# Whitening applied in 64x64 blocks with half-partition stores, and the first loads cut finer

## The chip, the cores and the metric

The kernel runs on one core of a Trainium2 chip. The core has a matrix engine (TensorE, PE in the profile), VectorE (DVE), ScalarE (ACT), GpSimd (POOL) and SyncE (SP), which here only issues DMA transfers. Data lie in SBUF, 128 partitions wide; products of PE arrive in PSUM, eight banks of 512 fp32 columns for each partition, and DVE or ACT copies them out ("eviction"). The metric is the time of one execution on the device in microseconds (us); smaller is better.

## The reference

The input x has 4 images of 256 channels and 64x64 pixels, fp32. Layer 0 computes 49 attention weights for each pixel and uses them to sum 49 shifted copies of x. Layer 1 whitens the result in 4 groups of 64 channels: mean and covariance over all images and pixels, five Newton steps towards an inverse square root, and one 64x64 matrix applied to each group.

```python
# layer 0
k = conv(x, w1, 7x7, dilation 2, padding 6) + b1        # w1: 128 x 256 x 7 x 7
k = conv(k, w2, 1x1) + b2                               # w2: 49 x 128
attn = softmax(k, axis=1)
xp = pad(x, 6)
shifts = stack([xp[:, :, 2*u:2*u+64, 2*v:2*v+64] for u in range(7) for v in range(7)], axis=1)
x = einsum('bkchw,bkhw->bchw', shifts, attn)
# layer 1, nc = 64 channels in a group, g = 4 groups
x = transpose(x, (1, 0, 2, 3)).reshape(g, nc, -1); m = x.shape[-1]
xc = x - x.mean(-1, keepdims=True)
Sigma = EPS * I + einsum('gdm,gem->gde', xc, xc) / m
rTr = (1.0 / einsum('gii->g', Sigma))[:, None, None]
Sigma_N = Sigma * rTr
P = I
for _ in range(5):
    P = 1.5 * P - 0.5 * (P @ P @ P) @ Sigma_N
xn = einsum('gde,gem->gdm', P * sqrt(rTr), xc)
out = xn * weight + bias                                # per channel
```

## The kernel before

Everything is fp32, and the stages follow one another with a good deal of overlap.

**Weights.** The two convolutions are merged: w2 times w1 gives a convolution from 256 channels straight to 49 taps. `w1` is loaded in four transfers (L183; two halves of 64 channels for each of the two channel blocks `cc` of 128), multiplied by `w2T` in 13 blocks of up to 10 channels (`CB`, L210; two products of 49 columns per block, one for each `cc`, into the two PSUM buffers `cv`) and evicted to `tapT`; each of the 49 taps is then transposed (L228) into `tap`. Evictions alternate between ACT and DVE (L202).

**First loads.** SP issues w1, then image 0 of x: even image rows into slot 0, odd rows into slot 1 (`load_x`, L129; four transfers of 1 MB, in rows of 256 bytes), then `gain` and `shift` (L191, L192). Every later store or load of SP stands behind these in SP's order, among them the store `gi` (L615) and the stores `gd` (L409). POOL clears some buffers once the weight pool is released, and then loads image 1 (slots 2 and 3, L129).

**Convolution.** The convolution of 7x7 taps is done by interpolation at 7 points in both directions (`row_eval`, `col_eval`, `conv_bank` at L491, `col_interp`, `row_interp`); some rows are convolved directly (`direct`, L597). Rows are handled in four phases: row `4q+a` of a slot belongs to phase `a`. For image 0 an order is written out by hand: DVE makes the first weights (`row_weights`, `weights`), then `row_eval(0, 1)`, which reads all four phases, then `col_eval`; PE does `direct0(INF, 0)`, which reads only phase 3 of both slots, then `direct0(0, 0)`, which reads phase 0, then the products of `conv_bank`. The transformed weights `wr` have one buffer for each of three banks of points, so DVE can write the next set only after PE has read the last.

**Attention, sum, moments.** Softmax, a move of the weights through DRAM into bands, the weighted sum (L926) and the moments (L976, into `sig`: 64x65 for each group) run under the convolution of the later images; a planner spreads them. Results of layer 0 stay in SBUF as the slots; three of them are spilled to DRAM and brought back at the end (`back`, L851).

**Whitening chain.** `whiten(cc)` runs for two halves of 128 channels, interleaved: two groups stand as two blocks on the diagonal of a 128x128 matrix. L1186 sums the diagonal by a product with the block matrix `blk`; `rtr` is its reciprocal, one number for each channel. The Newton steps are products of 128x128 (L1201, L1208). At the end `scale` holds gain times the square root of `rtr`, and `beta` comes from a product of the matrix with the mean (L1225).

**Apply** (L1246): for each image, half of the channels and 8 rows of a slot (512 columns), one product of the full 128x128 matrix; half of that matrix is zero. There are 64 products, one to each of three PSUM buffers `tp` in turn. The evictions multiply by `scale` and add `beta`, alternately on ACT (L1257) and DVE (L1261); two of them, for even and odd image rows, fill an `out` buffer of 128 partitions by 4 KB (four such buffers), and SP stores it in one transfer of 512 KB (L1265).

Of the kernel before, what the change touches and what calls it, by code (L numbers as in the profile page):

```python
# [9 lines left out]
F32 = mybir.dt.float32  # L10
AF = mybir.ActivationFunctionType
ALU = mybir.AluOpType
# [19 lines left out]
def kernel(  # L32
# [29 lines left out]
    nc = tc.nc  # L62
    B, C, H, W = x.shape
    P = 128
    NCC = C // P
# [4 lines left out]
    SH, SW = H // 2, W // 2  # L70
# [4 lines left out]
    GW = 64  # L75
# [15 lines left out]
    def pe(ins):  # L91
        return tc.keep_in_program_order(ins)

    const = ctx.enter_context(tc.tile_pool(name="const", bufs=1))
    work = ctx.enter_context(tc.tile_pool(name="work", bufs=2))
# [3 lines left out]
    ps_y = ctx.enter_context(tc.tile_pool(name="ps_y", bufs=1, space=bass.MemoryType.PSUM))  # L99
    ps_sg = ctx.enter_context(tc.tile_pool(name="ps_sg", bufs=1, space=bass.MemoryType.PSUM))  # L100

    def tp():
        return ps_tp.tile([P, 512], F32, tag="tp", name="tp")
# [18 lines left out]
    slots = {}  # L122
    store = []

    def load_x(s, k, queue):
        b, pr = divmod(k, 2)
        for cc in range(NCC):
            src = x[b, cc * P : (cc + 1) * P].rearrange("c (r two) w -> c r two w", two=2)
            queue.dma_start(store[s][:, cc], src[:, :, pr, :])  # L129
        slots[k] = store[s]  # L130
# [12 lines left out]
    nc.gpsimd.memset(b2_sb, 0.0)  # L143
    for h in range(2):
        nc.sync.dma_start(b2_sb[h * HB : h * HB + KT], b2.unsqueeze(1))
    gain_sb = const.tile([P, NCC], F32, name="gain_sb")
    shift_sb = const.tile([P, NCC], F32, name="shift_sb")

    w2T = w1p.tile([O1, P], F32, name="w2T")
    nc.gpsimd.memset(w2T, 0.0)  # L150
    t = tp()
# [3 lines left out]
    t = tp()  # L155
    nc.tensor.matmul(t[:, :1], w2T, b1_sb, start=True, stop=True)
    bias = const.tile([P, 1], F32, name="bias")
    nc.vector.tensor_tensor(bias, t[:, :1], b2_sb, ALU.add)

    cv_buf = []  # L160
    for k in range(2):
        t = ps_cv.tile([P, 512], F32, name=f"cv{k}")
# [13 lines left out]
    w1_sb = [w1p.tile([O1, P, KT], F32, name=f"w1_{cc}") for cc in range(NCC)]  # L176
# [1 line left out]
    tapT = w1p.tile([P, KT, P], F32, name="tapT")  # L178


    for c0 in range(0, P, P // 2):
        for cc in range(NCC):
            nc.sync.dma_start(  # L183
                w1_sb[cc][:, c0 : c0 + P // 2].rearrange("o c t -> o (c t)"),
                w1[:, cc * P + c0 : cc * P + c0 + P // 2].rearrange("o c u v -> o (c u v)"),
            )
    load_x(0, 0, nc.sync)
    load_x(1, 1, nc.sync)
    for cc in range(NCC):
        cs = slice(cc * P, (cc + 1) * P)  # L190
        nc.sync.dma_start(gain_sb[:, cc : cc + 1], gain[0, cs].rearrange("c a b -> c (a b)"))  # L191
        nc.sync.dma_start(shift_sb[:, cc : cc + 1], shift[0, cs].rearrange("c a b -> c (a b)"))  # L192


    n0, n3 = KS * NCC * 2 * KT, 3 * KS * NCC * KT
# [5 lines left out]
    def evict(k, o, i):  # L201
        (nc.vector.tensor_copy if k % 2 else nc.scalar.copy)(o, i)  # L202

    CB = 10
    for k, c0 in enumerate(range(0, P, CB)):
        n = min(CB, P - c0)
        t = cv_buf[k % 2]
        for cc in range(NCC):
# [5 lines left out]
                    start=True, stop=True,  # L214
# [8 lines left out]
    for k0 in range(0, KT, TB):  # L223
        n = min(TB, KT - k0)
        t = tp()
# [537 lines left out]
    for k in range(NY):  # L763
        a = bpool.tile([P, NCC, P // GW, GW + 1], F32, name=f"yt{k}")
# [369 lines left out]
                j += 1  # L1134
    apool.release()
    rpool = ctx.enter_context(tc.tile_pool(name="rp", bufs=1, reuse_waits="tile"))
    blk = rpool.tile([P, P], F32, name="blk")
    nc.gpsimd.memset(blk, 0.0)
    for g in range(P // GW):
# [10 lines left out]
    def square(name):  # L1150
        return bpool.tile([P, P], F32, tag="xb", name=name, bufs=4)

    wm, sc, beta = {}, {}, {}

    def whiten(cc):


        def evict(o, i):
            (nc.vector.tensor_copy if cc else nc.scalar.copy)(o, i)

        G = sig[:, cc]
        mu = work.tile([P, 1], F32, tag="mu", name=f"mu{cc}")
        nc.vector.tensor_scalar(mu, G[:, GW : GW + 1], 1.0 / NPIX, None, ALU.mult)
        D = square(f"D{cc}")
        nc.vector.tensor_scalar(D, ident, mu, None, ALU.mult)
        t = tp()
        nc.tensor.matmul(t[:, :P], blk, D, start=True, stop=True)
        nmu = work.tile([P, 1], F32, tag="nmu", name=f"nmu{cc}")
        nc.vector.tensor_scalar(nmu, mu, -1.0, None, ALU.mult)
        PS = rpool.tile([P, 2, P], F32, tag="PS", name=f"PS{cc}", bufs=2)  # L1170
        S = PS[:, 1]
        nc.vector.tensor_scalar(S, ident, EPS, None, ALU.mult)
        yield
        for g in range(P // GW):
            gs = slice(g * GW, (g + 1) * GW)
            nc.vector.scalar_tensor_tensor(
                S[gs, gs], G[gs, :GW], 1.0 / NPIX, S[gs, gs], ALU.mult, ALU.add
            )
        nc.vector.scalar_tensor_tensor(S, t[:, :P], nmu, S, ALU.mult, ALU.add)
        yield  # L1180
        dt_ = square(f"dt{cc}")
        nc.vector.tensor_tensor(dt_, S, ident, ALU.mult)
        dg = work.tile([P, 1], F32, tag="dg", name=f"dg{cc}")
        nc.vector.tensor_reduce(dg, dt_, AX.X, ALU.add)
        t = tp()
        nc.tensor.matmul(t[:, :1], blk, dg, start=True, stop=True)  # L1186
        yield
        rtr = work.tile([P, 1], F32, tag="rtr", name=f"rtr{cc}")
        nc.vector.reciprocal(rtr, t[:, :1])
        nc.vector.tensor_scalar(S, S, rtr, None, ALU.mult)  # L1190


        i15 = square(f"i15_{cc}")
        nc.vector.tensor_scalar(i15, ident, 1.5, None, ALU.mult)
        Pm = PS[:, 0]
        nc.vector.scalar_tensor_tensor(Pm, S, -0.5, i15, ALU.mult, ALU.add)
        yield

        for it in range(1, T_ITERS):
            t = tp()  # L1200
            nc.tensor.matmul(  # L1201
                t[:, : 2 * P], Pm, PS.rearrange("p a c -> p (a c)"), start=True, stop=True
            )
            sq = rpool.tile([P, 2, P], F32, tag="sq", name=f"sq{cc}_{it}", bufs=2)
            evict(sq.rearrange("p a c -> p (a c)"), t[:, : 2 * P])
            yield
            t = tp()
            nc.tensor.matmul(t[:, :P], sq[:, 0], sq[:, 1], start=True, stop=True)  # L1208
            nc.vector.tensor_scalar(Pm, Pm, 1.5, None, ALU.mult)
            yield  # L1210
            nc.vector.scalar_tensor_tensor(Pm, t[:, :P], -0.5, Pm, ALU.mult, ALU.add)
            yield


        q = work.tile([P, 1], F32, tag="q", name=f"q{cc}")
        nc.scalar.activation(q, rtr, AF.Sqrt)
        qi = work.tile([P, 1], F32, tag="qi", name=f"qi{cc}")
        nc.vector.reciprocal(qi, q)
        nc.vector.scalar_tensor_tensor(q, qi, rtr, q, ALU.mult, ALU.add)
        scale = work.tile([P, 1], F32, tag="scale", name=f"scale{cc}")  # L1220
        nc.vector.scalar_tensor_tensor(
            scale, q, 0.5, gain_sb[:, cc : cc + 1], ALU.mult, ALU.mult
        )
        t = tp()
        nc.tensor.matmul(t[:, :1], Pm, mu, start=True, stop=True)  # L1225
        yield
        bt = work.tile([P, 1], F32, tag="beta", name=f"beta{cc}")
        nc.vector.tensor_scalar(bt, t[:, :1], scale, -1.0, ALU.mult, ALU.mult)
        nc.vector.tensor_tensor(bt, bt, shift_sb[:, cc : cc + 1], ALU.add)
        wm[cc], sc[cc], beta[cc] = Pm, scale, bt  # L1230

    chains = [whiten(cc) for cc in range(NCC)]
# [1 line left out]
        pass  # L1234


    NT = 512
    TR = NT // W
    n = 0
    for b in (3, 2, 1, 0):  # L1240
        for cc in range(NCC):
            for q in range(SH // TR):
                st = rpool.tile([P, TR, 2, W], F32, tag="out", name=f"out_{b}_{cc}_{q}", bufs=4)
                for pr in range(2):
                    t = tp()
                    nc.tensor.matmul(  # L1246
                        t,
                        wm[cc],
                        slots[2 * b + pr][:, cc, q * TR : (q + 1) * TR, :].rearrange(
                            "p r w -> p (r w)"  # L1250
                        ),
                        start=True,
                        stop=True,
                    )
                    t3 = t.rearrange("p (r w) -> p r w", w=W)
                    if n % 2 == 0:
                        nc.scalar.activation(  # L1257
                            st[:, :, pr, :], t3, AF.Identity, bias=beta[cc], scale=sc[cc]
                        )
                    else:  # L1260
                        nc.vector.tensor_scalar(  # L1261
                            st[:, :, pr, :], t3, sc[cc], beta[cc], ALU.mult, ALU.add
                        )
                    n += 1
                nc.sync.dma_start(  # L1265
                    out[b, cc * P : (cc + 1) * P, 2 * q * TR : 2 * (q + 1) * TR, :],
                    st.rearrange("p r two w -> p (r two) w"),
                )


# [29 lines left out]
```

## Time and profile before

| | us |
|---|---|
| runs shown | 792.08, 794.63, 799.25 (median 794.63) |
| profiled execution, its own time | 793.55 |
| its span, first to last instruction | 791.8 |

| engine | busy us | share of the span | instructions |
|---|---|---|---|
| PE | 722.7 | 91% | 7444 |
| PE weight loads | 547.6 | 69% | 7444 |
| DVE | 625.9 | 79% | 1314 |
| ACT | 346.4 | 44% | 1018 |
| POOL | 34.1 | 4% | 46 |

The page gives busy time per engine, a chain of waits followed back from the last instruction, groups of instructions of one line ("operation output<-input, partitions x elements, xcount | busy, mean ns of one | idle before, and what ended it"), and DMA issues. An fp32 product appears as two records of matmul and two of weight load. The time line and the chain in order of time give "start us, length us, engine, line, operation, count", and in brackets the idle time before it and what ended that. A table by stage gives each engine's busy time in a stretch, the TensorE clock that was granted (1.00 is full), the mean busy share of the 16 DMA engines, and what they moved in GB/s. DMA moved 114.76 MB in all, at a mean of 145 GB/s; the times of its transfers are in the page's last part: the 32 stores of the output, 512 KB each, land 2.6 us after their issue (median), the four loads of w1 11.9 us, the four of image 0 22.8 us.

### The profile page before, as it was taken

Reading aid. Unit: us, or ns where it says so; the run is one execution under the profiler, and the core shown is the slowest. Engines: PE = TensorE matmul, PEld = TensorE weight load, DVE = VectorE, ACT = ScalarE, POOL = GpSimd, SP = SyncE. Lnnn points to the kernel's source line nnn. Section 1 sums busy time; section 2 is a strip of 40 time slices with the busy share of each in tenths; the row PEclk is TensorE's granted clock in tenths of the full one; section 3 lists DMA queues with packets and bytes.
Section 4 is the critical chain, followed back from the end, with each engine's and each line's share of the span. In section 5 each row is a group of like instructions: output and inputs, shape, how many; then the busy total and the mean of one; then the engine's idle time right before and its main releaser. Section 6 shows DMA issues by size and latency. Waiting matters only on the chain.

```text
span 791.8 us, 18445 instructions
## 1 busy us (share of the span) xinstructions
PE 722.7 (91%) x7444; PEld 547.6 (69%) x7444; DVE 625.9 (79%) x1314; ACT 346.4 (44%) x1018; POOL 34.1 (4%) x46
## 2 busy tenths in 40 slices
PE   4899969799799999989999999896999889998997
PEld 1349653265688887768899958795998768875443
DVE  2696999999888999979896899696979775545443
ACT  1313241125674444378543344765333573422443
POOL 0320000030000010001000100000000000000000
PEclk9999989999899999999999999998999999998999
DMA  8991110033654383048644720542431233381676
GB/s 331 226 297 58 42 72 36 0 107 121 187 182 147 114 313 81 19 153 265 202 124 147 247 66 8 155 161 84 143 87 30 48 113 126 106 298 53 265 301 283
DMA packets 58717, 114.76 MB, mean 145 GB/s; under 512 B 22615, under 2 KB 41736, under 8 KB 57352
## 3 DMA queue, kind: packets, MB, share of 16 engines
q1 hardware_dynamic: 54936, 94.71, 36.2%
q0 software_dynamic: 3696, 18.88, 7.1%
q8 instruction: 59, 0.97, 0.5%
q14 instruction: 26, 0.21, 0.1%
HBM read 66.23 MB, written 47.33 MB: 143 GB/s over the span
## 4 chain that ended last, share of the span: by engine, by line
PE 36%; DVE 29%; ACT 12%; DMA 5%; issue 4%; SPq 1%; DVEq 0%; ACTq 0%
PE y L926 11%; PE cv L491 8%; PE tp L1246 7%; ACT zt L837 6%; DMA sd<-zt 4%; DVE xh L296 3%; PE sig L976 3%; PE tp L897 3%; PE tp L955 3%; DVE zz L296 3%; DVE pv L296 2%; DVE rb L289 2%; ACT d L794 2%; DVE ct L296 2%; DVE pv L292 2%
## 5 line engine op out<-in xcount | busy, mean ns | idle before, releaser
L491 PE MATMUL cv<-xh,wr 128*49 128x128 f32 x4368 | 251.6, 276 | 6.6 <-DVE xh L296 6.5
L491 PEld LDWEIGHTS cv<-xh,wr 128*49 128x49 f32 x4368 | 245.3, 124 | 11.5 <-issue 9.1
L926 PE MATMUL y<-band,xb 128*128 128x224 f32 (+2 forms) x640 | 156.0, 383 | 17.4 <-ACT xb L905 15.2
L926 PEld LDWEIGHTS y<-band,xb 128*128 128x128 f32 x640 | 112.3, 198 | 40.2 <-ACT xb L905 18.1
L837 ACT COPY zt<-d 32x112 f32<-32x112 f32 (+1 forms) x224 | 62.8, 281 | 22.1 <-DMA sd<-zt 13.8
L897 PE MATMUL tp<-ident,slot 128*128 128x128 f32 x256 | 51.1, 303 | 15.0 <-ACT yt L963 15.0
L963 ACT COPY yt<-tp 128x256 f32<-128x256 f32 x128 | 45.4, 375 | 36.7 <-PE tp L955 35.7
L945 ACT ACTIVATE slot<-y,pivot 128x512 f32<-128x512 f32 x53 | 36.5, 736 | 52.3 <-PE y L926 52.3
L501 ACT COPY pv<-cv 113x486 f32<-113x486 f32 (+1 forms) x63 | 29.8, 473 | 63.7 <-PE cv L491 62.4
L897 PEld LDWEIGHTS tp<-ident,slot 128*128 128x128 f32 x256 | 40.3, 206 | 22.3 <-ACT yt L963 16.7
L955 PE MATMUL tp<-ident,slot 128*128 128x128 f32 x256 | 52.2, 300 | 3.6 <-ACT xb L905 1.2
L879 DVE STREAM_TRANSPOSE band<-band 128x960 f32<-128x960 f32 (+1 forms) x48 | 50.9, 1059 | 5.8 <-DMA band<-sd 5.7
L955 PEld LDWEIGHTS tp<-ident,slot 128*128 128x128 f32 x256 | 41.5, 205 | 13.6 <-issue 4.4
L1261 DVE TENSOR_SCALAR out<-tp,scale,beta 128x512 f32<-128x512 f32 x32 | 25.9, 810 | 29.5 <-PE tp L1246 29.5
L794 ACT ACTIVATE d<-tp,mx 128x49 f32<-128x49 f32 x128 | 36.9, 336 | 12.2 <-DVE mx L789 12.1
L1257 ACT ACTIVATE out<-tp,beta,scale 128x512 f32<-128x512 f32 x32 | 24.9, 778 | 32.0 <-PE tp L1246 32.0
L296 DVE SCALAR_TENSOR_TENSOR xh<-ct 128x512 f32<-128x512 f32 x42 | 27.9, 686 | 12.6 <-PE cv L491 12.4
L976 PE MATMUL sig<-yt 128*64 128x65 f32 x1024 | 37.5, 227 | 0.0
L976 PEld LDWEIGHTS sig<-yt 128*64 128x64 f32 x1024 | 33.0, 140 | 6.0 <-issue 4.5
L1246 PE MATMUL tp<-slot,PS 128*128 128x512 f32 x80 | 35.9, 593 | 0.0
L905 ACT COPY xb<-tp 128x256 f32<-128x256 f32 x87 | 30.6, 374 | 12.0 <-PE tp L897 11.2
L597 PE MATMUL cv<-slot,wi 128*49 128x496 f32 (+3 forms) x168 | 34.7, 570 | 0.0
(203 smaller groups left out, 991.7 us busy)
## 6 DMA issues: line engine op xcount, KB each, us to landing
out_dram<-out SPq DMA_DIRECT2D x32, 512.0 KB, 2.6
sd<-zt SPq DMA_DIRECT2D x16, 896.0 KB, 4.3
slot<-in_x_dram POOLq DMA_DIRECT2D x12, 1024.0 KB, 10.0
band<-sd SPq DMA_DIRECT2D x128, 84.0 KB, 2.1
wr<-gd SPq DMA_DIRECT2D x15, 588.0 KB, 4.0
wr<-gd SPq DMA_DIRECT2D x15, 490.0 KB, 3.5
w<-in_L_conv_w_dram SPq DMA_DIRECT2D x4, 1568.0 KB, 11.9
spill<-slot POOLq DMA_DIRECT2D x3, 2048.0 KB, 7.8
```

The costliest lines, as they stand in the source:

```text
L296: return in_turn(STT(o, a, f, b, ALU.mult, ALU.add))
L491: nc.tensor.matmul(cv[h * HB : h * HB + KT, k, sr : sr + n, sc : sc + n], wv[:, sc, sr, cc], xh[bc][:, :n, h * NCC + cc, :n], start=(j == ...
L794: nc.scalar.activation(d[:, h, i], lt[i // NI][:, i % NI, h, :KT], AF.Exp, bias=mx[:, i, h : h + 1], accum_out=s[:, h, i : i + 1],)
L837: nc.scalar.copy(o, i)
L879: nc.vector.transpose(f, f)
L897: nc.tensor.transpose(t[:, cc * P : (cc + 1) * P], xt[:, cc, CR * m : CR * (m + 1), bass.ds(pc, SW, 2)], ident,)
L926: nc.tensor.matmul(ps[:, cc, q0 - half * HALF : q1 - half * HALF, :], xb[:, cc * P : (cc + 1) * P], rhs, start=(k == 0), stop=(k == len(PI ...
L945: nc.scalar.activation(o, ps[:, cc], AF.Identity, bias=pivot[:, cc : cc + 1])
L955: nc.tensor.transpose(t[:, cc * P : (cc + 1) * P], yt[:, cc, CR * i : CR * (i + 1), bass.ds(pc, SW, 2)], ident,)
L963: nc.scalar.copy(yb.rearrange("p a g c -> p (a g) c")[:, :, :GW], t[:, :C].rearrange("p (e c) -> p e c", c=GW),)
L976: nc.tensor.matmul(sig[g * GW : (g + 1) * GW, cc], yb[:, cc, g, :GW], yb[:, cc, g], start=(count[0] == 0 and cc == 0), stop=(count[0] == 4 ...
L1246: nc.tensor.matmul(t, wm[cc], slots[2 * b + pr][:, cc, q * TR : (q + 1) * TR, :].rearrange("p r w -> p (r w)"), start=True, stop=True,)
```

## The change

1. **First weights.** w1 comes in five parts of 30, 30, 30, 20 and 18 channels for each `cc`, ten transfers for four.
2. **x of image 0** comes by row phases, phase 3 first, then 0, 1 and 2: 16 transfers of 256 KB for four of 1 MB.
3. **gain and shift** are laid out for groups of 64 channels (64 channels by 4 groups, twice, once for each half of the partitions) and are loaded by POOL's queue, ahead of POOL's clearing of buffers.
4. **Whitening chain.** `scale` and `beta` become 128x2 (one column for each group of the half, the same in both halves of the partitions). For that, the diagonal sum of each group is spread over all partitions by a product with a matrix of ones (`dgg`, `tg`, `rg`), and the product with the mean is made of four 64x64 products.
5. **Apply.** For 16 rows of a slot and both groups of a half, four products of 64x64 by 512 columns: group `g` reads partitions `64g` to `64g+63`, and 8-row piece `h` writes partitions `64h` to `64h+63` of bank `g`. So a bank holds one group, with its first 8 rows in the lower partitions and the next 8 in the upper. Three pairs of banks are used in turn (the former `y`, `cv`, and two `tp`). Evictions stay 128 partitions by 512. There are six `out` buffers for four, and each is stored in two transfers of 64 partitions, 256 KB.

```diff
-    for c0 in range(0, P, P // 2):
+    CB = 10
+    for c0, c1 in ((0, 3), (3, 6), (6, 9), (9, 11), (11, 13)):
+        c0, c1 = c0 * CB, min(c1 * CB, P)
         for cc in range(NCC):
             nc.sync.dma_start(
-                w1_sb[cc][:, c0 : c0 + P // 2].rearrange("o c t -> o (c t)"),
-                w1[:, cc * P + c0 : cc * P + c0 + P // 2].rearrange("o c u v -> o (c u v)"),
-            )
-    load_x(0, 0, nc.sync)
-    load_x(1, 1, nc.sync)
-    for cc in range(NCC):
-        cs = slice(cc * P, (cc + 1) * P)
-        nc.sync.dma_start(gain_sb[:, cc : cc + 1], gain[0, cs].rearrange("c a b -> c (a b)"))
-        nc.sync.dma_start(shift_sb[:, cc : cc + 1], shift[0, cs].rearrange("c a b -> c (a b)"))
+                w1_sb[cc][:, c0:c1].rearrange("o c t -> o (c t)"),
+                w1[:, cc * P + c0 : cc * P + c1].rearrange("o c u v -> o (c u v)"),
+            )
+
+    for pr in range(2):
+        slots[pr] = store[pr]
+    for a in (3, 0, 1, 2):
+        for pr in range(2):
+            for cc in range(NCC):
+                nc.sync.dma_start(
+                    store[pr][:, cc].rearrange("c (q a) w -> c a q w", a=4)[:, a],
+                    x[0, cc * P : (cc + 1) * P].rearrange(
+                        "c (q a two) w -> c two a q w", two=2, a=4
+                    )[:, pr, a],
+                )
+    for h in range(2):
+        hs = slice(h * GW, (h + 1) * GW)
+        for t, src in ((gain_sb, gain), (shift_sb, shift)):
+            nc.gpsimd.dma_start(t[hs], src[0].rearrange("(g c) a b -> c (g a b)", c=GW))
...
+        dgg = work.tile([P, P // GW], F32, tag="dgg", name=f"dgg{cc}")
+        nc.vector.tensor_scalar(dgg, blk[:, ::GW], dg, None, ALU.mult)
+        tg = tp()
+        nc.tensor.matmul(tg[:, : P // GW], ones, dgg, start=True, stop=True)
         rtr = work.tile([P, 1], F32, tag="rtr", name=f"rtr{cc}")
         nc.vector.reciprocal(rtr, t[:, :1])
         nc.vector.tensor_scalar(S, S, rtr, None, ALU.mult)
+        rg = work.tile([P, P // GW], F32, tag="rg", name=f"rg{cc}")
+        nc.vector.reciprocal(rg, tg[:, : P // GW])
...
-        nc.vector.scalar_tensor_tensor(q, qi, rtr, q, ALU.mult, ALU.add)
...
-        nc.tensor.matmul(t[:, :1], Pm, mu, start=True, stop=True)
+        nc.vector.tensor_tensor(qi, qi, rg, ALU.mult)
+        nc.vector.tensor_tensor(q, qi, q, ALU.add)
...
+        ts = [tp() for g in range(G2)]
+        for g in range(G2):
+            gs = slice(g * GW, (g + 1) * GW)
+            for h in range(2):
+                nc.tensor.matmul(
+                    ts[g][h * GW : (h + 1) * GW, :1], Pm[gs, gs], mu[gs],
+                    start=True, stop=True, skip_group_check=True,
+                )
...
+    def banks():
+        while True:
+            t = ps_y.tile([P, G2, NT], F32, tag="y", name="apply")
+            yield [t[:, g] for g in range(G2)]
+            yield cv_buf
+            yield [tp() for g in range(G2)]
...
-                    nc.tensor.matmul(
-                        t,
-                        wm[cc],
-                        slots[2 * b + pr][:, cc, q * TR : (q + 1) * TR, :].rearrange(
-                            "p r w -> p (r w)"
-                        ),
...
+                    ts = next(pair)
+                    for h in range(2):
+                        for g in range(G2):
+                            gs = slice(g * GW, (g + 1) * GW)
+                            pe(
+                                nc.tensor.matmul(
+                                    ts[g][h * GW : (h + 1) * GW],
+                                    wm[cc][gs, gs],
+                                    slots[2 * b + pr][
+                                        gs, cc, (q + h) * TR : (q + h + 1) * TR, :
+                                    ].rearrange("p r w -> p (r w)"),
...
-                nc.sync.dma_start(
-                    out[b, cc * P : (cc + 1) * P, 2 * q * TR : 2 * (q + 1) * TR, :],
-                    st.rearrange("p r two w -> p (r two) w"),
-                )
+                for g in range(G2):
+                    c0 = cc * P + g * GW
+                    for h in range(2):
+                        r0 = 2 * (q + h) * TR
+                        nc.sync.dma_start(
+                            out[b, c0 : c0 + GW, r0 : r0 + 2 * TR, :],
+                            st[g][h * GW : (h + 1) * GW].rearrange("p r two w -> p (r two) w"),
+                        )
```

## The prediction

> **What bounds the kernel now.** I read the page first: its chain of waits puts 36% of the span on TensorE (PE), 29% on VectorE (DVE), 12% on ScalarE (ACT), 5% on DMA. The diff touches only the two ends of the span, so I then read the chain in order of time and the time line there. Last stage, from the chain:
>
> ```profile
> 731.22 0.02 issue
> 731.24 0.30 DVE PS L1211
> 731.54 0.04 issue
> 731.59 0.38 PE tp L1225 x2
> 731.97 55.06 PE tp L1246 x128
> 787.03 0.03 issue
> 787.05 0.81 DVE out L1261
> ```
>
> One unbroken piece of PE is 55.06 us. 64 products of 128x128 by 512 columns make 128 records (two passes each), so a product costs 0.86 us. What runs beside it, from the table by stage (PE, PEld, DVE, ACT, POOL busy, clock, DMA share, GB/s) and the page's groups:
>
> ```profile
> 744.00:748.00 4.00, 4.00 (x11) 1.83 (x10) 2.05 (x3) 1.66 (x3) 0.00 (x0) 1.00 0.76 312
> 748.00:752.00 4.00, 4.00 (x10) 1.71 (x9) 2.00 (x3) 1.65 (x3) 0.00 (x0) 1.00 0.79 323
> L1261 DVE TENSOR_SCALAR out<-tp,scale,beta 128x512 f32<-128x512 f32 x32 | 25.9, 810 | 29.5 <-PE tp L1246 29.5
> L1257 ACT ACTIVATE out<-tp,beta,scale 128x512 f32<-128x512 f32 x32 | 24.9, 778 | 32.0 <-PE tp L1246 32.0
> ```
>
> DVE and ACT are half idle and wait for PE; DMA is next in line, three quarters busy.
>
> Start, from the time line:
>
> ```profile
> 12.98 13.59 PE L210 MATMUL cv<-w,w2T 128*49 128x490 f32 x50 [1.86 <-DMA w<-in_L_conv_w_dram]
> 32.99 1.92 PE L597 MATMUL cv<-slot,tap 128*49 128x512 f32 x6
> 37.18 11.64 PE L597 MATMUL cv<-slot,tap 128*49 128x512 f32 x48 [2.28 <-DMA slot<-in_x_dram]
> 60.81 23.03 PE L491 MATMUL cv<-xh,wr 128*49 128x128 f32 x409
> 66.41 0.36 DVE L289 TENSOR_TENSOR wr<-ct 128x196 f32<-128x196 f32 x1 [5.47 <-PE cv L491]
> ```
>
> PE gets its first full pair of weight parts at 12.98, although DMA has been full since 4 us. It does three products of the direct convolution at 33, then stands until x arrives at 37.18. The last line counts most: DVE, busy without a gap from 29.7 to 61, waits 5.47 us for PE, since its next weights go into a buffer that PE is reading. So up to 66.4 **PE leads and DVE has 5.5 us of slack**; from there to about 145 DVE leads.
>
> [...] The trace shows column pairs only: in the direct convolution (L597) two products of 49 columns take 0.80 us together, as one does. In steps of 10 ns, two of its records begin in the same step at 32.99, so the second product doesn't wait for the second pass of the first. No row tile is in the trace. [...] The change gives each channel group its own bank. [...] No 64-partition store is in the trace. [...] 439 GB/s while the weights load, and stretches at 426 to 442 inside single stores.
>
> **The change part by part.**
>
> *First weights.* Ten transfers of 0.45 to 0.75 MB replace four of 1.6 MB; the same 6.4 MB. The last byte lands near 20.4 as now (6.4 MB at 430 GB/s from 4.2 us = 19.1, plus 1.3 to land: a 512 KB store lands 2.6 us after issue, half of that is its bytes). Part one (1.5 MB) is there at about 8.8 instead of 12.98. Now 13 column blocks at 0.86 to 1.05 us each follow 12.98 and end at 27.1. Then, only the two blocks of part five lie after the last byte: 20.4 + 2 x 0.86 + 0.5 eviction = 22.7; if the first blocks run at a low clock, as the first does now (1.9 us), 23.5. I take **3.8 us earlier** for the L228 transposes and for DVE's weight sums behind them. Six more issues on SP at about 0.46 us lie under 15 us of transfers.
>
> *gain and shift.* Four issues leave SP, where they stand between 29.76 and 36.8 ahead of the gi and gd stores, for POOL, which is idle from 1.5 to 33. Their 1,024 four-byte elements fall among the first weights. An x row of 256 B costs an engine 15 ns (16,384 rows in 15.5 us over 16 engines); at that price 64 elements per engine delay the weights by 1 us. Bounds 0 and 2; inside the 3.8.
>
> *x by row phases.* 16 transfers of 256 KB for four of 1 MB, the same 256 B rows in another order. x moves at 280 GB/s: phase 3, which the first direct convolution needs, lands near 25, phase 0 near 29, all near 37 as now. POOL's loads for image 1 start about 4 us earlier, at 34, and overlap the end by a microsecond or two. DVE's row_eval needs all four phases and would start at 42.3 - 3.8 = 38.5: just covered. If x is late, DVE loses its 3.8, but not PE.
>
> *PE at the start.* Transposes end at 33.0 - 3.8 = 29.2. The 112 records of the two direct convolutions at 0.405 us a pair are 22.7 us, without the wait and without the half clock (0.50 at 38 to 40) after it. L491 begins at 51.9 instead of 60.81: 8.9 earlier. PE frees the weight buffer at 57.5, DVE is there at 61.0 - 3.8 = 57.2. So **8.5 us** of 66.4 go; 5.5 if DVE doesn't move at all, 9.5 at best. Instruction order behind this is the same on PE, DVE, POOL and SP, and ACT's early shifts (the acc eviction ahead of an xh copy) cover work needed only later, so I let the gain run through.
>
> *Whitening chain* (715.2 to 732). Added per half: a 128x2 multiply, a 128x128 product with one eviction, a 128x2 reciprocal in front of the first PS; at the end four 64x64 products for one, and three small DVE operations for two. L1186 took 0.40 us from product to DVE read, a small DVE operation 0.15 to 0.2. One product round and some four of these on the path, and a wait for the fourth of three tp banks: **1.3 us** more, bounds 0.3 and 2.5. The two sets of scale operations lie under the iteration.
>
> *Apply.* 128 products of 64x64, four in 0.86 us if all run at once: 32 x 0.86 = 27.6 us of PE for 55.1. Evictions stay 32 x 0.81 on DVE, 32 x 0.78 on ACT, 26 us each. SP issues 64 stores: 64 x 0.33 (a store's issue now) = 21 us. So DMA becomes the bound: 16.78 MB. A share of 0.76 at 312 GB/s means 410 at full share: 40.9 us. Before that, two rounds of PE, an eviction and the way to the first byte: 1.7 + 0.8 + 0.9 = 3.4 us; after the last byte 1.8 (now 790.0 to 791.8); a microsecond for gaps: 47.0 us. Now, from 731.8 to 791.8, it is 60.0. **13.0 us** less; bounds: 440 GB/s gives 15, 350 gives 7. Six output buffers at 1.28 us of transfer each hold 7.7 us, their round of two evictions, issue and landing is about 5, so they don't hold DMA up.
>
> Sum: -8.5 + 1.3 - 13.0 = **-20.2** on the profiled execution of 793.55 us (span 791.8 plus 1.75 around it): 773.4. It lies 1.1 under the median of 794.63, so I forecast **774.5**.
>
> **Rivals.** *A, row tiles don't run at once* (the change doesn't do what it says): pairs of columns alone make 64 x 0.86 = 55 us of PE again. The apply stage is then as now: 794.6 - 8.5 + 1.3 = 787. For: no row tile in the trace. Against: the independence of column tiles at 32.99[...]. *B, the start's gain is given back* before 145 us, or x comes late enough to hold PE too: 794.6 + 1.3 - 13.0 = 783. For: DVE and PE have less than a microsecond between them then. Against: 5.5 us of slack in DVE's wait. *C, slower: stores of 64 partitions move at half the rate*, 205 GB/s. Apply is 3.4 + 82 + 2 = 87 us for 60: 794.6 - 7.2 + 27 = 814. Break-even is an apply stage of 67 us, 271 GB/s; under 240 it is over 1% slower. For: the 32-partition band loads reach only 197 GB/s at a share of 0.8. Against: those are 84 KB each with short rows, paced by an issue of 0.42 us; the store keeps its 4 KB rows.
>
> **How the numbers follow.** Main case 0.63, B 0.14, A 0.12, C 0.07, rest 0.04. Main case's own bounds: 794.6 - 9.5 + 0.3 - 15 = 770 to 794.6 - 5.5 + 2.5 - 7 = 785. The range 769 to 788 takes in A and B and leaves out C. One per cent (7.9 us) is what can be told from no change: 786.7 divides. Faster: main, B, rest and a little of A: 0.82; same: 0.11; slower: 0.07.
>
> **What would show it.** Transposes ending near 29; no wait of PE for x; DVE's wait of 5.5 at L289 gone to below 1; L491 starting near 52; the apply products in about 28 us of PE work but spread over 43 by waits for evictions, with DVE and ACT waiting for the stores' buffers, and a DMA share near 1 at over 400 GB/s. Wrong if PE still runs without a gap through the apply stage (A), or if DMA shows a share near 1 at half the GB/s (C).

## The result, and the profile after

The changed kernel takes 828.99 us (median of 4 runs, 825.91 to 830.77) against 793.95 for the kernel before beside it: ratio 1.0426, 95% interval 1.0365 to 1.0487. It is slower by 4%, where 774.5 us was forecast. The profiled execution took 825.91 us, span 824.1.

Four points on the time line show where the time went: the first product of conv_bank, the first operation of whitening (mu), the first eviction of the apply stage, the end of the span.

| us | before | after | stage before | stage after | difference |
|---|---|---|---|---|---|
| conv_bank's first product | 60.0 | 66.5 | 60.0 | 66.5 | +6.5 |
| whitening begins | 716.4 | 741.0 | 656.4 | 674.5 | +18.1 |
| first apply eviction | 733.0 | 758.5 | 16.6 | 17.5 | +0.9 |
| end | 791.8 | 824.1 | 58.8 | 65.6 | +6.8 |

More than half of the loss lies in the long middle, which the diff doesn't touch. The start first, from the time lines of TensorE (PE), then VectorE (DVE) of the changed kernel (start, duration, engine, line, operation, count, idle time before it and what ended that):

```profile
9.74 13.76 PE L223 MATMUL cv<-w,w2T 128*49 128x490 f32 x50 [1.17 <-DMA w<-in_L_conv_w_dram]
29.91 11.59 PE L610 MATMUL cv<-slot,tap 128*49 128x512 f32 x56
41.33 11.55 PE L610 MATMUL acc<-slot,tap 128*49 128x512 f32 x56
66.47 8.73 PE L504 MATMUL cv<-xh,wr 128*49 128x128 f32 x106 [13.60 <-DVE xh L302]
```

```profile
59.58 2.36 DVE L302 TENSOR_TENSOR rb<-slot 128x1024 f32<-128x1024 f32 x2 [18.00 <-DMA slot<-in_x_dram]
```

PE did what was planned: weights from 9.74, both direct convolutions without a gap from 29.91. Then DVE stood for 18 us on x, and PE for 13.6 us on DVE. The DMA records between 40 and 44 us show what x was up against (packets, MB and share of 16 engines by queue; q0 is POOL's, q1 is SP's):

```profile
DMA packets 626, 0.87 MB, mean 217 GB/s; under 512 B 441, under 2 KB 441, under 8 KB 626
q0 software_dynamic: 197, 0.76, 86.4%
q1 hardware_dynamic: 429, 0.11, 18.9%
```

POOL is loading image 1 in records of about 4 KB, while the last rows of image 0 go by in 256 B: seven bytes of image 1 for one of image 0. From 46 to 48 us it is 99 records of 4096 B on POOL's queue against 99 of 256 B on SP's, from 46 to 58 us 630 against 637 in all, and the last part of image 0 lands only at 59.5. So x of image 0 had not come in before POOL started: its rate was 219 GB/s where the kernel before has 280 (between 24 and 30 us, first line before, second after):

```profile
DMA packets 6584, 1.68 MB, mean 280 GB/s; under 512 B 6584, under 2 KB 6584, under 8 KB 6584
```

```profile
DMA packets 5149, 1.31 MB, mean 219 GB/s; under 512 B 5148, under 2 KB 5148, under 8 KB 5148
```

The end: the chain of waits, then the table by stage (PE, PEld, DVE, ACT, POOL busy, clock, DMA share, GB/s), an eviction group and the list of DMA issues:

```profile
806.00 1.06 SPq L1327
...
807.15 0.69 SPq L1327
...
807.90 4.35 DMA out_dram<-out
```

```profile
764.00:768.00 4.00, 2.65 (x28) 0.84 (x24) 1.90 (x3) 1.52 (x3) 0.00 (x0) 1.00 0.84 275
768.00:772.00 4.00, 2.11 (x24) 0.71 (x20) 1.53 (x2) 1.43 (x2) 0.00 (x0) 1.00 0.84 269
```

```profile
L1318 DVE TENSOR_SCALAR out<-cv,scale,beta 128x512 f32<-128x512 f32 x11 | 8.8, 804 | 8.9 <-DMA out_dram<-out 8.9
```

```profile
out_dram<-out SPq DMA_DIRECT2D x64, 256.0 KB, 4.1
```

PE is no longer the bound: it is busy 2.1 to 2.7 us in each 4 and the evictions wait for stores. But the stores move 270 GB/s, not 410, and the chain runs through SP, where one issue takes 0.545 to 1.299 us (median 0.887) instead of 0.332. The 64 issues take 55.6 us in all and follow one another, from 760.1 to 819.6, with no pause over 0.3 us.

### The profile page after: what moved, and what is told of

Same layout as the page of the kernel before. It is cut to its first block, busy times and chain, and to the rows that moved or that the text cites. A ratio compares the mean times of both kernels' runs of the same rounds, so it can differ in the third digit from the quotient of the medians.

```text
span 824.1 us, 18802 instructions
## 1 busy us (share of the span) xinstructions
PE 712.7 (86%) x7588; PEld 539.5 (65%) x7588; DVE 625.7 (76%) x1322; ACT 344.6 (42%) x1018; POOL 36.8 (4%) x51
## 4 chain that ended last, share of the span: by engine, by line
PE 36%; DVE 24%; ACT 11%; SPq 6%; DMA 6%; issue 4%; DVEq 0%; ACTq 0%
PE y L939 13%; PE cv L504 11%; ACT zt L850 5%; SPq L1327 5%; DMA sd<-zt 3%; PE sig L989 3%; PE tp L910 3%; PE tp L968 3%; DVE xh L309 3%; DVE zz L309 2%; ACT d L807 2%; DMA band<-sd 2%; DVE pv L309 2%; DVE ct L309 1%; PE cv L610 1%
## 5 line engine op out<-in xcount | busy, mean ns | idle before, releaser
L504 PE MATMUL cv<-xh,wr 128*49 128x128 f32 x4368 | 254.9, 279 | 21.6 <-DVE xh L302 15.1
L504 PEld LDWEIGHTS cv<-xh,wr 128*49 128x49 f32 x4368 | 248.7, 126 | 26.5 <-ACT xh L475 14.4
L939 PE MATMUL y<-band,xb 128*128 128x224 f32 (+2 forms) x640 | 163.2, 397 | 18.6 <-ACT xb L918 16.4
L939 PEld LDWEIGHTS y<-band,xb 128*128 128x128 f32 x640 | 116.7, 205 | 44.1 <-ACT xb L918 19.4
L958 ACT ACTIVATE slot<-y,pivot 128x512 f32<-128x512 f32 x53 | 36.5, 734 | 59.6 <-PE y L939 59.5
L514 ACT COPY pv<-cv 113x486 f32<-113x486 f32 (+1 forms) x63 | 29.8, 473 | 71.8 <-PE cv L504 65.4
L968 PEld LDWEIGHTS tp<-ident,slot 128*128 128x128 f32 x256 | 41.5, 206 | 13.7 <-issue 4.5
L309 DVE SCALAR_TENSOR_TENSOR pv<-pv 113x162 f32<-113x162 f32 x105 | 33.7, 321 | 1.0
L302 DVE TENSOR_TENSOR rb<-slot 128x1024 f32<-128x1024 f32 x16 | 19.0, 1217 | 18.0 <-DMA slot<-in_x_dram 18.0
L918 DVE COPY xb<-tp 128x256 f32<-128x256 f32 x41 | 16.4, 421 | 21.1 <-PE tp L910 21.0
## 6 DMA issues: line engine op xcount, KB each, us to landing
slot<-in_x_dram POOLq DMA_DIRECT2D x12, 1024.0 KB, 12.3
```

The costliest lines, as they stand in the source:

```text
L309: return in_turn(STT(o, a, f, b, ALU.mult, ALU.add))
L504: nc.tensor.matmul(cv[h * HB : h * HB + KT, k, sr : sr + n, sc : sc + n], wv[:, sc, sr, cc], xh[bc][:, :n, h * NCC + cc, :n], start=(j == ...
L918: (nc.vector.tensor_copy if tail else nc.scalar.copy)(xb, t[:, :C])
L939: nc.tensor.matmul(ps[:, cc, q0 - half * HALF : q1 - half * HALF, :], xb[:, cc * P : (cc + 1) * P], rhs, start=(k == 0), stop=(k == len(PI ...
L968: nc.tensor.transpose(t[:, cc * P : (cc + 1) * P], yt[:, cc, CR * i : CR * (i + 1), bass.ds(pc, SW, 2)], ident,)
```

## The experiments

The first theory, S, was that the start is the culprit: x by row phases, overtaken by image 1. Its rival was the apply part. Two runs take the change apart, two more try repairs.

**Start alone.** The kernel before with the new start:

```
+    (w1 in five parts, x of image 0 by row phases, as in the change)
-        nc.sync.dma_start(gain_sb[:, cc : cc + 1], ...)
+        nc.gpsimd.dma_start(gain_sb[:, cc : cc + 1], ...)
```

> The kernel before with the new start alone: weights in five parts, x of image 0 by row phases, gain and shift from POOL (in their old layout). Theory S (the start is what costs most): the second half of row_eval waits for x until about 59.6 us, as in the changed kernel, and the whitening chain begins at about 739 instead of 715; time 817 us, +23 to +25. Rival L (most is lost in the last stage or in the middle): time within 5 us of 794.

Measured: ratio 0.9905, interval 0.9874 to 0.9936; conv_bank begins at 53.3, whitening at 710.7. Theory S falls: the start with which conv_bank begins 6.5 us later in the changed kernel lets it begin 6.7 us earlier here.

**Whitening and apply alone.** The changed kernel with the old start:

```
-    for c0, c1 in ((0, 3), (3, 6), (6, 9), (9, 11), (11, 13)):   (new start)
+    for c0 in range(0, P, P // 2):                                (old start)
```

> The changed kernel with the old start: weights in four parts, x as before, gain and shift from SP. Theory S: start as before, row_eval without a wait for x, whitening chain at 715 to 716; the last stage as in the changed kernel, 66.6 us for 60.0 and one more in the chain, so 802 us, +7 to +9. Rival L: 815 or more.

Measured: 1.0292 (1.0212 to 1.0372). And this was the puzzle: with the *old* start conv_bank begins at 64.2, and the middle is slow as well. From the first to the third quarter of conv_bank's products takes 286 us here and in the changed kernel, 273 before and 272 in the start alone. Something in the whitening and apply parts, code that runs after 716 us, slows transfers at 25 us.

**Old x order and two store queues; image 1 behind image 0.**

```
-                        nc.sync.dma_start(
+                        (nc.sync, nc.gpsimd)[h].dma_start(      (x in the old order)
```

> The changed kernel with two edits at its two ends: x of image 0 in its old order (weights still in five parts), and the stores of the upper partition half issued from POOL. Start: if the row phases' slower reading (215 GB/s for 280) is what lets image 1's loads catch up, x is in by 37 to 39 us, row_eval's second half starts at 39 to 42, whitening chain at 707 to 711. If image 1's loads starve x whenever they start 3 us earlier, row_eval's second half waits until 45 or later. End: if SP's issue of 0.93 us per store is the bound, two queues of 32 stores give over 380 GB/s and an apply stage of 46 to 51 us. If transfers of 64 partitions are slow on the DMA engines, the stage stays at 64 to 67 us and 270 GB/s.

```
+    for s in range(2, 4):
+        load_x(s, s, nc.sync)          (after image 0; not from POOL)
+    (512 KB stores: both channel groups of a partition half in one)
```

> The changed kernel with two edits at its two ends: image 1's loads issued by SP behind image 0's (same queue), x by row phases kept; and one store of 512 KB for both groups of a partition half (64 partitions, two rows of 4 KB each, 32 stores). Start: if two queues sharing the engines packet by packet starve x, then without the second queue x is in by 40 to 42 at 215 GB/s, row_eval's second half starts there, whitening chain at 709 to 714. If reading by phases is slow by itself, it waits to 50 or later. End: if the cost is per issue on SP, 32 issues of 0.9 us give 46 to 51 us of apply at over 380 GB/s. If it goes by the row or by the partition half, an issue takes 1.8 us or the engines stay at 270 GB/s, and the stage at 64 to 67 us.

Single executions: 810.13 and 801.69 us. With image 1 queued behind image 0, conv_bank begins at 53.0 although x still moves at 220 GB/s, so the overtaking is real and accounts for 13 us. With x in its old order conv_bank begins at 64.6. But the middle stays slow in both (283 and 285 us). Neither the order of x nor the queues explains it.

**The place of the tiles.** What can code at the end change at 25 us? The addresses. The new tiles dgg and rg are two new tags in the pool `work` with two buffers each; a buffer takes 32 bytes per partition, so 128 in all, and everything allocated behind that pool moves by as much. In the built programs, slot0 begins at byte 26880 of each partition before (105 x 256) and at 27008 after (105.5 x 256); the other slots, zz, rb, out and the rest likewise. The start alone has the old addresses, the three other runs the new. Hence theory P, with a run for each direction:

```
+    pad = const.tile([P, 32], F32, name="pad")     (128 bytes, in the changed kernel)
+    nc.gpsimd.memset(pad, 0.0)
```

> The changed kernel with an unused constant of 128 bytes per partition added, so that the slots and everything behind them begin on multiples of 256 bytes in the on-chip memory again, as in the kernel before (the two new small tiles of the whitening, dgg and rg, had moved them by 128). Instructions and their order are those of the changed kernel. Theory P (the place of the tiles): x of image 0 arrives at about 280 GB/s instead of 215, the first products of conv_bank begin at about 53 us instead of 66.5, conv_bank goes from its first to its third quarter in 272 us instead of 285, whitening begins at about 711 us; the apply stage stays at 60 to 67 us; span 789 to 796, ratio to the kernel before 0.990 to 1.005. Theory Q (the place is nothing; image 1's early loads slow x, and a lower granted clock slows the middle): span 820 to 828, conv_bank from 66 us, 285 us in the middle, as the changed kernel has them.

```
+    pad = const.tile([P, 32], F32, name="pad")     (128 bytes, in the kernel before)
+    nc.gpsimd.memset(pad, 0.0)
```

> The kernel before with an unused constant of 128 bytes per partition, so that all its slots and output tiles begin 128 bytes past a multiple of 256. Nothing else changes. Theory P: x by POOL lands in 12.3 us instead of 10.0, the first products of conv_bank begin at about 64 instead of 60, its middle half takes 285 instead of 273 us, whitening begins at about 736 instead of 716; the stores read misplaced tiles too, and the apply stage takes 60 to 66 us; span 810 to 820, ratio 1.02 to 1.035. Theory Q: nothing changes, 792 us, ratio within 0.5% of 1.

Measured: the changed kernel with 128 unused bytes comes to 0.9996 (0.9974 to 1.0018), the kernel before with 128 unused bytes to 1.0258 (1.0199 to 1.0317). One constant takes 34.5 us off one span (824.1 to 789.6) and puts 15.2 on the other (791.8 to 807.0). Of the 34.5 us, 13.1 lie ahead of conv_bank, 19.5 between its first product and whitening, 1.9 in the apply stage. The kernel before, where image 1 starts later, loses 3.2 ahead of conv_bank and 13.0 between the two. In the first, PE's time line at the start reads

```profile
30.57 11.59 PE L612 MATMUL cv<-slot,tap 128*49 128x512 f32 x56
41.99 11.55 PE L612 MATMUL acc<-slot,tap 128*49 128x512 f32 x56
53.36 21.91 PE L506 MATMUL cv<-xh,wr 128*49 128x128 f32 x390
```

with no wait left between the direct convolutions and conv_bank; whitening begins at 708.4. In the second the DMA records from 24 to 30 us, and the loads of x by POOL (10.0 us before), read

```profile
DMA packets 5145, 1.31 MB, mean 219 GB/s; under 512 B 5145, under 2 KB 5145, under 8 KB 5145
```

```profile
slot<-in_x_dram POOLq DMA_DIRECT2D x12, 1024.0 KB, 12.5
```

Its apply stage is 58.8 us as before, where 60 to 66 were expected: a 512 KB store from a tile that lies 128 bytes off costs nothing here, a load of 256-byte rows into one does.

**Which tiles, and is it 128?**

```
+    pad                                            (ahead of the slots)
+    pads ahead of w2_sb, zz and blk                (all others back on multiples of 256)
```

> The kernel before with only its five slots 128 bytes past a multiple of 256 (a pad ahead of them, and pads that bring everything allocated behind them back to multiples of 256). It tells whether it is the x rows, which x is loaded into, that cost the time. Theory S (the x rows alone): x by POOL lands in 12.4 us, whitening begins at about 733 as with everything shifted, span 805 to 809, ratio 1.02 to 1.03. Theory O (other tiles, such as rb, wr, zz and the tiles that come back from DRAM, have their share): x lands in 12.4 us but whitening begins between 719 and 729, span 795 to 803, ratio 1.004 to 1.017.

```
+    pad = const.tile([P, 16], F32, name="pad")     (64 bytes)
```

> The kernel before with everything 64 bytes past a multiple of 256 instead of 128. Theory R (a row of 256 bytes that crosses a 256-byte boundary is what costs): as with 128, x by POOL lands in 12 to 13 us, whitening begins at about 733, ratio 1.02 to 1.03. Theory M (it needs 128[...]): 10.0 us, ratio within 0.5% of 1.

Measured: 1.0207 (1.0159 to 1.0254) and 1.0203 (1.0153 to 1.0253); POOL's x lands in 12.2 and 12.4 us, whitening begins at 735.4 and 729.8. The slots alone cost as much as everything, and 64 bytes as much as 128. Could it be that the engines read the slots more slowly there? They don't: between the kernel before and the kernel shifted by 128, VectorE's `rb<-slot` of 1024 columns takes 1217 ns in both, PE's transposes of the slots 301 and 302 ns on the mean. What is left is the loading of x: in all shifted kernels each row of 256 B crosses a 256-byte boundary.

**Why the middle, too.** Images 0 and 1 are in by 65 us, yet the loss grows to 700. The shifted kernel before, in the middle, against the kernel before at the same place (time line, then table by stage); before:

```profile
393.05 3.18 PE L926 MATMUL y<-band,xb 128*128 128x320 f32 x12 [0.66 <-ACT xb L905]
```

```profile
390.00:398.00 8.00, 7.34 (x68) 6.06 (x69) 8.00 (x15) 4.76 (x13) 0.00 (x0) 1.00 0.40 109
```

shifted:

```profile
400.10 0.51 PE L899 MATMUL tp<-ident,slot 128*128 128x128 f32 x2 [2.17 <-ACT yt L965]
401.63 4.87 PE L928 MATMUL y<-band,xb 128*128 128x320 f32 x12 [0.74 <-ACT xb L907]
```

```profile
400.00:408.00 8.00, 7.16 (x52) 5.30 (x52) 8.00 (x21) 3.19 (x8) 0.00 (x0) 0.79 0.07 17
```

The same twelve records take 3.18 us in one and 4.87 in the other, where the granted clock is 0.79 on the mean of the stretch: after PE's pauses it stands at half from 402.5 to 405.9. The shifted kernel has such a dip at 400, 472 and 512 us, the kernel before none at the same places.

The pause at 400 can be followed back. PE waits for an eviction `yt` on ScalarE, which stands behind ScalarE's copies `zt`; these wait for a store of SP (`sd`) to land. It lands 8.6 us after its issue instead of 5.5, while POOL's loads of x are still under way (the second of two lands 12.5 us after its issue instead of 9.6). First the kernel before, then shifted:

```profile
384.80 3.79 ACT L837 COPY zt<-d 32x112 f32<-32x112 f32 x13 [3.46 <-DMA sd<-zt]
```

```profile
393.40 3.79 ACT L839 COPY zt<-d 32x112 f32<-32x112 f32 x13 [6.04 <-DMA sd<-zt]
```

The other pauses were not followed one by one. Between the same two VectorE operations (211.2 to 528.1 before, 215.9 to 543.3 shifted) the span grows by 10.5 us, PE's busy time with the same products by 6.0 of them; the rest is waiting. The middle half of conv_bank divides in the same way in all fifteen traces. With the slots at their old place PE stands idle for 10.9 to 12.9 us of it, with the slots shifted for 16.3 to 18.5; half clock lasts 7 to 14 us and 14 to 24. PE's busy time goes with the clock, from 260 us where half clock lasts 6.8 to 268 where it lasts 23.9. So late rows make short pauses, and the clock makes them dearer. The clock's part differs from one execution to the next (13.7 us occur in both groups); the idle time of the two groups doesn't overlap. The kernels at the old alignment need 271 to 277 us for the middle half of conv_bank, those shifted 281 to 286; the two groups don't overlap.

**The stores.** In the profiled execution of the realigned kernel whitening begins 8.0 us earlier than in the kernel before, and the apply stage gives most of it back: 63.8 us from first eviction to end. Two cuts of the old stores in the kernel before:

```
+    for h in range(2):     64 partitions each, packets of 4 KB
+        nc.sync.dma_start(out[b, c0 + h * GW ...], st[hs]...)
```

> The kernel before with each 512 KB store cut into two, one for each half of the partitions: 64 stores of 256 KB over 64 partitions in packets of 4 KB, as the changed kernel issues them, on tiles at their old places. Theory H (a store of 64 partitions is slow in itself: SP takes 0.93 us for its issue against 0.33, and 64 of them are 59.5 us): the apply stage goes from 60 to 65 to 68 us, span 797 to 800, ratio 1.006 to 1.010. Theory P alone (the changed kernel's stores were slow because their tiles lay 128 bytes off): apply stays at 60 us with issues of about 0.33 us, ratio within 0.3% of 1.

```
+    for h in range(2):     128 partitions each, packets of 2 KB
+        nc.sync.dma_start(out[..., r0 : r0 + TR, :], st[:, h * (TR // 2) ...])
```

> The kernel before with each 512 KB store cut by rows instead: 64 stores of 256 KB over all 128 partitions, packets of 2 KB. Theory H: the issue stays at about 0.33 us and the apply stage at 60 us, ratio within 0.3% of 1; if it is the number of stores that counts, or the smaller packet, apply goes to 64 to 68 us as in the cut by partition halves, ratio 1.005 to 1.010.

Measured: 1.0133 (1.0085 to 1.0182), stage 65.4 us; and 0.9998 (0.9963 to 1.0032), stage 58.9. Same number of stores, same bytes: it is the partition half. SP's issues, first by halves, then by rows:

```profile
L1267 SPq DMA_DIRECT2D out_dram<-out x64: 467/805/1706, 737.3 to 795.9; - x64
```

```profile
L1267 SPq DMA_DIRECT2D out_dram<-out x64: 332/407/1308, 732.3 to 785.9; - x64
```

Is SP's issue the limit, or what the DMA does with such a store? The realigned kernel with its upper halves on POOL, as in the run with two queues above:

```
+    pad = const.tile([P, 32], F32, name="pad")
-                        nc.sync.dma_start(
+                        (nc.sync, nc.gpsimd)[h].dma_start(
```

> The realigned changed kernel with its stores of the upper partition half issued by POOL. Theory H2 (a half store costs DMA time per byte, 46.9 us of an engine per MB in the run with two queues): 16.8 MB over 16 engines are 49 us, the apply stage takes 55 to 57 us, span 780 to 783, ratio 0.983 to 0.990. Theory I (it is SP's issue of 0.79 to 0.93 us that binds): with half of the stores on another queue the stage falls to 46 to 50 us, span 771 to 776, ratio 0.970 to 0.982.

Measured: 0.9902 (0.9877 to 0.9927), stage 55.7. For the stage H2 holds (a half store costs the DMA more time per byte); the whole lies just above its range, and in the profiled execution whitening begins only at 716.0, with twice the half clock of the realigned kernel in the middle half (13.7 us for 6.8). SP's 32 issues now take 1.40 us each (median) where 64 took 0.79: an issue has no fixed price here, and SP is occupied nearly all the time in both. In the first run with two queues (stage 56.4 us, between the two outcomes that were expected) the DMA share was 0.97 at 333 GB/s (758 to 802 us): the engines are full, and a 4 KB packet takes them 192 ns. Reckoned likewise (share x 16 engines x time / packets' bytes), it is 160 ns before and 200 ns in the changed kernel. So two limits lie one behind the other: one queue of 256 KB stores fills the engines to 0.84, and full they reach some 330 GB/s (merged into 512 KB stores on one queue, in the run with image 1 behind image 0: share 0.99 at 319 GB/s, stage 59.3 us).

**Whole-partition stores with four products.** The two products that keep their partition half go to one bank, the two that swap to another, whose halves are moved home by the eviction:

```
+    gs, k = slice(g * GW, (g + 1) * GW), int(g != h)
+    nc.tensor.matmul(ts[k][h * GW : (h + 1) * GW], wm[cc][gs, gs], ...(q + k)...)
+    for k, lo, n_, to in ((0, 0, P, 0), (1, 0, GW, GW), (1, GW, GW, 0)):
+        evict ts[k][lo : lo + n_] to st[k][to : to + n_]
+    nc.sync.dma_start(out[b, cc * P : (cc + 1) * P, ...], st[k])
```

> The realigned changed kernel with its four 64x64 products dealt out otherwise: the two that keep their partition half write one bank for one block of rows, the two that swap write the other bank for the next block. The first bank is evicted as one, the second in two halves that are written back to their own partitions, so that each tile holds 128 channels and goes out in one store of 512 KB over all partitions, 32 stores as in the kernel before. 96 evictions instead of 64. Theory H (what held the apply stage at 65 us was the store of one partition half, 47 to 49 us of a DMA engine per MB against 39): SP issues take about 0.33 us, the DMA moves 360 to 400 GB/s, the apply stage takes 46 to 50 us, span 771 to 776, ratio 0.970 to 0.982. Theory E (the 96 evictions of 0.77 to 0.81 us, on two engines 38 us, or the products themselves bind): apply 52 to 60 us, span 777 to 786, ratio 0.982 to 0.995.

Measured: 0.9898 (0.9857 to 0.9938), stage 57.5. SP's issues are back at 332 ns and a packet at 160 ns, but the DMA share is only 0.77 (740 to 780 us): E was right in the time, though no engine was full. The time line shows ScalarE and VectorE waiting 0.8 to 1.0 us for each other's write to the same tile. Last, each tile's evictions from one engine:

```
-                        if n % 2 == 0:
+                        if (k + q // 2) % 2 == 0:
```

> The kernel with whole-partition stores, with the evictions dealt out by tile: all writes of one output tile (two whole banks, or four halves) come from one engine, ScalarE and VectorE in turn by tile, so that no engine waits for the other's write to the same tile (in the run before, the two waited 0.8 to 0.97 us for each other in each round of evictions). Theory E1 (these waits set the pace of 1.65 us per pair of banks): six evictions of 0.8 us per MB on two engines are 2.4 us, the DMA's 2.45 us per MB at 410 GB/s comes out equal, the apply stage falls from 57 to 46 to 49 us, span 772 to 777, ratio 0.970 to 0.980. Theory E2 (the waits are only where the stage's slack lies, and the four products in 64x512 pieces, 2.6 to 3.6 us busy in each 4, set it): 55 to 57 us, span 783 to 786, ratio 0.987 to 0.992.

Measured: 782.22 us, 0.9844 (0.9803 to 0.9886), stage 52.0. Table by stage:

```profile
744.00:748.00 4.00, 2.83 (x25) 0.80 (x18) 3.80 (x5) 2.28 (x4) 0.00 (x0) 1.00 0.96 390
748.00:752.00 4.00, 2.78 (x30) 0.73 (x23) 3.90 (x6) 2.95 (x4) 0.00 (x0) 1.00 0.80 330
752.00:756.00 4.00, 2.62 (x25) 0.86 (x18) 3.46 (x5) 2.80 (x5) 0.00 (x0) 1.00 0.97 397
```

It lies between E1 (46 to 49) and E2 (55 to 57): the waits were worth 5.5 us. What sets the pace after that was not separated: VectorE is busy for 3.8 of 4 us in some stretches, but from 732 to 774 us VectorE and ScalarE are both busy for 0.78 of the time and the DMA for 0.88. Its ratio is the lowest of all, and it beats both kernels.

## Why the prediction was wrong

The 773.4 us forecast for the profiled execution were missed by 52.5: by 15.0 at the start, 18.1 in the middle, 19.8 in the apply stage and -0.4 in whitening. The realigned kernel takes back 34.5 of them; the rest is the apply stage.

- **First weights**: right in kind, a little large. Transposes were to end 3.8 us earlier, at 29.2; direct convolution starts at 29.91, 3.1 earlier, and realigned at 30.57.
- **x by row phases**: the failing step, first half. "x moves at 280 GB/s" was read from the kernel before and carried over to slots at other addresses: 219 (row phases at the old addresses: 265 to 267). "POOL's loads overlap the end by a microsecond or two" became 21 us, from POOL's first records at 38.4 to the last of image 0 at 59.5, and "DVE loses its 3.8, but not PE" became a wait of 13.6 us on PE. With the slots put back, the step is right: conv_bank begins at 53.36 for 51.9. What of it reaches whitening differs from one execution to the next: in the five kernels with the new start and the old alignment whitening begins 0.4 to 8.6 us earlier than before, 6.3 at the median, where 8.5 was forecast.
- **"Instruction order is the same, so I let the gain run through"**: the failing step, second half: +18.1 us in the middle where 0 was put. The order is the same; the tiles' places aren't, and all twelve loads of x by POOL pay for it, 12.3 us each for 10.0. Neither the page nor the diff's lines on dgg and rg say so; only the addresses do.
- **Whitening**: +1.3 forecast, +0.9 measured.
- **Apply, -13.0 forecast, +6.8 measured** (5.0 realigned). PE's part, where four products at once were the author's estimate (no trace of before shows a row tile), was right: eight records of four products take 1.04 us, and the next eight start 0.86 us later, so rival A is out.

```profile
768.05 1.04 PE L1299 MATMUL cv<-slot,PS 64*64 64x512 f32 x8
768.91 1.04 PE L1299 MATMUL tp<-slot,PS 64*64 64x512 f32 x8
```

  Two terms were mis-sized: "64 x 0.33 = 21 us" of issues are 55.6, and "410 at full share" is 330, neither of which holds for 64 partitions. Rival C named the right place at the wrong rate: 270 GB/s (283 realigned) for its 205, about its break-even of 271. Alone it makes no kernel slower by 4%, and the realigned kernel, which has it, is level with the kernel before.
- **Rivals**: none was "a new small tile moves the slots". The range of 769 to 788 left out every such case.

The rates give the price of a shifted row, as an estimate (256 B x 16 engines / rate): 18.7 ns of one engine at the 219 GB/s above instead of 14.6 at 280. Stores read from shifted tiles in 4 KB packets show none: in the kernel shifted by 128 they take SP 332 ns to issue and land after 2.6 us (medians), as before. Two stores over half of the partitions each, which the forecast put at the price of one over all, lose 1.3% here (1.0133).

## What to carry to other kernels

Before costing a diff by its instructions, compare where the tiles lie: a few bytes more in an early pool move everything behind it, and here rows of 256 B loaded into tiles 64 or 128 bytes off a 256-byte multiple came in about a quarter more time (12.2 to 12.5 us for 10.0). If transfers or products far from the edit slow down with the same instruction order, suspect the addresses first, and test it with a pad in both kernels. A store's price is read from a store over the same partitions; where a rearrangement for one engine halves the partitions, keeping the output tiles whole and letting the eviction move the halves home paid here (0.9844 against 0.9996).

## What was not expected of the hardware

- 64 or 128 bytes of shift of the slots cost 2.0 to 2.6% of the whole kernel; a shift by 256 (the realigned kernel, middle half 271 us for 273) none.
- A store over 64 partitions takes SP 0.47 to 0.59 us to issue at the beginning of the apply stage (0.33 over 128), up to 1.7 later in it, and its 4 KB packets take 192 to 200 ns for 160. Why wasn't found.
- TensorE's clock fell to half after pauses of 2 to 3 us in all (2.17 + 0.74 at 400, above). The length of a pause does not decide it: one of 1.37 us at 233.1 in the kernel before is followed by a dip, the same one in the shifted kernel (1.39 us) is not, nor is one of 2.48 + 0.60 us in the kernel before. Stretches of half clock last 3.4 us or a whole multiple in all fifteen traces (3.413, 6.827, 10.240 and 17.067 us in those of the kernel before and the changed kernel), unless the end of the kernel cuts them off. What exactly trips it stays open.
